# Written order on VectorE, ScalarE and Pool between two expert FFNs, with the routing in six pieces

## The chip, the cores and the metric

One core of one Trainium2 chip runs the kernel. The metric is device time in microseconds (us). TensorE is PE in the profile, VectorE DVE, ScalarE ACT, GpSimd POOL, and the engine that issues most transfers SP. Weight loads of TensorE have a row of their own, PEld.

## The reference

4096 tokens (16 sequences of 256) of width 256, all in float32. The layer is a macaron:

```
x = x + 0.5 * ffn(layernorm(x))     # first FFN
x = x + attention(layernorm(x))
x = x + 0.5 * ffn(layernorm(x))     # second FFN, same weights

ffn(h):  n = w_norm * rms_norm(h)
         probs = softmax(n @ w_router)               # 32 experts, top 4, 128 slots each
         each expert: (silu(g) * u) @ w_down         # hidden width 176
         shared:  sigmoid(n @ w_sg) * ((silu(n @ sw_gate) * (n @ sw_up)) @ sw_down)   # hidden width 704
         return h + weighted experts + shared
attention: 16 query heads, 8 key/value heads of 32, rotary, 50*tanh(s/50), causal softmax
```

## The kernel before

x stays in SBUF as 32 tiles of 128 tokens; four tiles make a **group**, so there are eight groups. The stages, in the order in which they are written:

- **First FFN, routing.** `route(n, g)` (L209) is a generator that is advanced piece by piece. `moments` (L197) takes mean and variance (DVE `st`, `mv`) and a power on POOL (`s`). Then come the normalised rows `xr` (DVE, L230), the rescaled residual `x` (ACT, L233, which overwrites what `xr` reads), transposes `pt` on PE, their copies `xnT` (ACT), router logits `pl` (PE), `lg` and `ex` (DVE, ACT), and the top-4 chain from `tot` to `mask` (DVE, L262 to L279) with a write of `xr` to the DRAM table `xtab` (SP). `rows` has two buffers for `xr`.
- **Slots** (L284) turn the masks into token indices; **experts** (L369) gather rows, run three products and scatter-add into the DRAM sum `acc`.
- **Sums and projections.** `project(pool, g)` (L427) reads `acc` back (`a`, one buffer), adds it to x on POOL (L423), takes the moments, normalises (`h`, ACT, L443), transposes (`pta`, PE), and makes q, k and v: six products `pq` (PE, L456), each turned by a shuffle `qs` and a product with the cosines on DVE (L459, L463; `qs` has two buffers) and two operations on POOL (L464, L465), and two products `pv` copied to `v` by DVE (L488).
- **Attention** is a loop over **units** `k = 4g + j`, j = 0..3: group g, one of its two sequences, one half of the heads. A unit issues wide scores `sc` (PE), tanh and exp on ACT (L512, L515), a causal select on POOL (L517); for odd j the output product `poa` and its addition to x (DVE, L560); some projection products of group g+1; narrow scores `sc`; then denominators `den` and values `y` of the unit before, whose DVE steps run from `dT` to `yT` (L541 to L546). Scores and the shared FFN's `pg` live in one PSUM pool, `big`, of two buffers: a unit's narrow scores wait for the tanh of its wide ones. Most other products use the pool tag `mm`, also two buffers.
- **Fill.** The shared FFN (`shared`, L332: `pg` on PE, tanh on ACT, two steps `act` on DVE, `po` on PE) has no deadline. `fill.take(us)` issues that many us of it wherever PE would wait; the constants on L44 say how much.
- **Second FFN**, as the first; the routing of groups 0 to 6 is advanced inside the attention loop.

The order of instructions on PE is the written one (`manual_schedule`, L95). On DVE, ACT, POOL and SP a scheduler has chosen it when the program was built. [...]

In the attention loop, per group, the pieces stand as follows (before): routing of group g-1 in j = 1 (moments), j = 2 and j = 3 (xr, x and transposes, half each), and of g-2 in j = 0 (logits) and j = 1 (top-4 chain). Group g+2's projection: j = 1 sum, j = 2 moments, j = 3 `h` and transposes. Group g+1's products: j = 0 three `pq`, j = 1 two `pv`, j = 2 three `pq`.

The lines that the order turns on:

```
ORDERED = {mybir.EngineType.PE}
ROUTE_FILL, SLOT_FILL, FIRST_FILL, EXPERT_FILL, SUM_FILL, PROJECT_FILL = 2.2, 2.5, 6.0, 2.4, 14.0, 2.0
SPARE = (1.0, 0.0, 3.0, 4.0)
PROJECT_PIECES = ((2, 1), (0, 2), (2, 1), (0, 0))
```

Of the kernel before, what the change touches and what calls it, by code (L numbers as in the profile page):

```python
# [13 lines left out]
ALU = mybir.AluOpType  # L14
# [22 lines left out]
QK_SCALE = 256.0 ** -0.5  # L37
TINY = float(np.finfo(np.float32).tiny)
XW = C + E
ORDERED = {mybir.EngineType.PE}  # L40

ROUTE_FILL, SLOT_FILL, FIRST_FILL, EXPERT_FILL, SUM_FILL, PROJECT_FILL = 2.2, 2.5, 6.0, 2.4, 14.0, 2.0  # L44
SPARE = (1.0, 0.0, 3.0, 4.0)
PROJECT_PIECES = ((2, 1), (0, 2), (2, 1), (0, 0))

# [40 lines left out]
def macaron_kernel(ctx: ExitStack, tc: tile.TileContext, X, Wq, Wk, Wv, Wo, w_norm, w_router, w_gate, w_up,  # L88
# [3 lines left out]
    of = out.rearrange("b t c -> (b t) c")  # L92


    ctx.enter_context(tc.manual_schedule(engines=ORDERED))  # L95
    cpool = ctx.enter_context(tc.tile_pool(name="consts", bufs=1))
    dram = ctx.enter_context(tc.tile_pool(name="dram", bufs=1, space=DRAM))
    stat = ctx.enter_context(tc.tile_pool(name="stat", bufs=3))
# [97 lines left out]

    def moments(g):  # L197

        mv = stat.tile([P, GT, 2], F32, name="mv")
        for t in range(GT):  # L200
            st = stat.tile([P, 6], F32, name="st")
            nc.vector.bn_stats(st, x[:, g * GT + t, :])
            nc.vector.bn_aggr(mv[:, t, :], st)
        s1 = stat.tile([P, GT], F32, name="s1")
        nc.gpsimd.tensor_scalar_add(s1, mv[:, :, 1], LN_EPS)
        nc.gpsimd.tensor_tensor(s1, s1, power, ALU.pow)
        return mv, s1

    def route(n, g):  # L209

        mv, s1 = moments(g)
        s2 = stat.tile([P, GT], F32, name="s2")
        nc.gpsimd.tensor_mul(s2, s1, s1)
        nc.gpsimd.tensor_mul(s2, s2, mv[:, :, 1])
        nc.gpsimd.tensor_scalar_add(s2, s2, RMS_EPS)
        nc.gpsimd.tensor_tensor(s2, s2, power, ALU.pow)
        nc.gpsimd.tensor_mul(s2, s2, s1)
        xa = stat.tile([P, GT], F32, name="xa")
        nc.gpsimd.tensor_scalar(xa, s1, 0.5, 1.0, ALU.mult, ALU.add)
        xb = stat.tile([P, GT], F32, name="xb")  # L220
        nc.gpsimd.tensor_mul(xb, s1, mv[:, :, 0])
        nc.gpsimd.tensor_scalar_mul(xb, xb, -0.5)
        xr = rows.tile([P, GT, XW], F32, name="xr")
        yield 0.0
        for h in range(GT // 2):
            pt = ps1.tile([P, 2, 2, P], F32, tag="mm", name="pt")
            for j in range(2):
                t = 2 * h + j
                i = g * GT + t
                nc.vector.tensor_scalar(  # L230
                    xr[:, t, 0:C], x[:, i, :], mv[:, t, 0:1], s2[:, t : t + 1], ALU.subtract, ALU.mult
                )
                nc.scalar.activation(  # L233
                    x[:, i, :], x[:, i, :], AF.Identity, bias=xb[:, t : t + 1], scale=xa[:, t : t + 1]
                )
                for c in range(2):
                    nc.tensor.transpose(pt[:, c, j, :], xr[:, t, c * P : (c + 1) * P], ident)
            i0 = (g * GT + 2 * h) * P
            for c in range(2):
                nc.scalar.activation(  # L240
                    xnT[:, c, i0 : i0 + 2 * P], pt[:, c].rearrange("p j t -> p (j t)"), AF.Identity,
                    scale=wnorm[:, c : c + 1],
                )
            yield 0.5
        pl = ps1.tile([P, GT, E + 1], F32, tag="mm", name="pl")
        for t in range(GT):
            i = g * GT + t
# [36 lines left out]
    def slots(pool, idx, q):  # L284
# [6 lines left out]
            nc.tensor.matmul(pc[:NT, e, :], lhsT=mask[:, q * EG + e, :], rhs=triu, start=True, stop=True)  # L291
        cum = pool.tile([NT, EG, P + 1], F32, name="cum")
        nc.scalar.copy(cum[:, :, 0:P], pc[:NT])
        cnt = pool.tile([NT, EG], F32, name="cnt")
        nc.vector.tensor_copy(cnt, cum[:, :, P - 1])
        yield 0.5
# [14 lines left out]
        nc.vector.tensor_tensor(past, iota, hi.unsqueeze(2).to_broadcast([NT, EG, CAP]), ALU.is_ge)  # L311
        nc.gpsimd.tensor_sub(sel, sel, past)
        nc.vector.tensor_add(cum[:, :, 0:P], cum[:, :, 0:P], lo.unsqueeze(2).to_broadcast([NT, EG, P]))
        nc.vector.tensor_copy(cum[:, :, P : P + 1], const("base", NT).unsqueeze(1).to_broadcast([NT, EG, 1]))
        yield 0.2
        row = pool.tile([P, EG], F32, name="row")
        for e0 in range(0, EG, 3):
# [109 lines left out]
    def project(pool, g):  # L427


        add_sums(g, read_sums(pool, 0, g, 1))  # L430
        yield 0.0
        mv, s1 = moments(g)
        hb = stat.tile([P, GT], F32, name="hb")
        nc.gpsimd.tensor_mul(hb, s1, mv[:, :, 0])
        nc.gpsimd.tensor_scalar_mul(hb, hb, -1.0)
        yield 0.0
        hT = pool.tile([P, 2, GW], F32, name="hT")
        for p in range(GT // 2):
            pt = ps1.tile([P, 2, 2, P], F32, tag="mm", name="pta")
            for j in range(2):  # L440
                t = 2 * p + j
                h = rows.tile([P, C], F32, name="h")
                nc.scalar.activation(  # L443
                    h, x[:, g * GT + t, :], AF.Identity, bias=hb[:, t : t + 1], scale=s1[:, t : t + 1]
                )
                for c in range(2):
                    nc.tensor.transpose(pt[:, c, j, :], h[:, c * P : (c + 1) * P], ident)
# [150 lines left out]
    def feed_forward(n, pool, works, fill):  # L598


        for g in works:
            fill.take(ROUTE_FILL)
            next(works[g])
            if g + 1 in works:
                next(works[g + 1])
            for _ in works[g]:
                fill.take(ROUTE_FILL)
            fill.ready = g + 1
        if n == 0:
            clear(0)  # L610
# [16 lines left out]
    proj = ExitStack()  # L627
    with tc.tile_pool(name="ffn0", bufs=1) as pool:
        first = {g: route(0, g) for g in range(NG)}
        next(first[0])  # L630
        feed_forward(0, pool, first, fill)
        clear(1)
        pp = proj.enter_context(tc.tile_pool(name="proj", bufs=1, side="right", reuse_waits="tile"))
        projects = {0: project(pp, 0)}
        next(projects[0])
        fill.take(SUM_FILL)
        next(projects[0])
        fill.take(FIRST_FILL)
        for _ in projects[0]:
            fill.take(PROJECT_FILL)  # L640
        fill.finish(2)
        projects[1] = project(pp, 1)
        for _ in range(4):
            next(projects[1])
            fill.take(PROJECT_FILL)

    def store(i, tiles=1):
        nc.sync.dma_start(
# [15 lines left out]
    with tc.tile_pool(name="attn", bufs=1, reuse_waits="tile") as pool:  # L664
# [5 lines left out]
        for k in range(len(units) + 2):  # L670
# [18 lines left out]
            spare_time(SPARE[j])  # L689
            advance(projects.get(g + 1), PROJECT_PIECES[j][1])  # L690

            if j < 2 and g >= 2:
                advance(routing[g - 2])
                fill2.ready = g - 2 + j
            elif j >= 2:
                advance(routing.get(g - 1))
            if j == 1:
                if g >= 1:
                    routing[g - 1] = route(1, g - 1)
                    next(routing[g - 1])  # L700
                if g + 2 < NG:
                    projects[g + 2] = project(pp, g + 2)
                    next(projects[g + 2])
            if j == 2 and g + 2 < NG:
                fill.finish(g + 3)
                next(projects[g + 2])
            if j == 3:
                advance(projects.get(g + 2), 2)
    proj.close()

    with tc.tile_pool(name="ffn1", bufs=1, reuse_waits="tile") as pool:
# [36 lines left out]
```

## Time and profile before

| what | value |
|---|---|
| three runs | 1242.18, 1249.54 (median), 1250.28 us |
| profiled execution | 1249.98 us, span on the core 1248.3 us |
| mean granted TensorE clock | 0.958 |
| DVE busy | 615.6 us (49%) |
| ACT busy | 419.4 us (34%) |
| POOL busy | 501.9 us (40%) |
| chain that ended last | PE 73%, DVE 10%, POOL 6%, ACT 4%, DMA 4% |

The span can be cut by what PE works on: routing 0 to 123 us, slots to 235, experts to 403, sums and first projections to about 463, attention to 920, the second FFN's slots to 1040, its experts and the end to 1248. Idle time of an engine counts only where another one, in the end PE, waits for it.

### The profile page before, as it was taken

How to read it: one execution, taken by the hardware profiler on the slowest of the kernel's cores; microseconds unless marked ns; L12 is line 12 of the kernel's file. 1: busy time of each engine (PE TensorE's matmuls, PEld its weight loads, DVE VectorE, ACT ScalarE, POOL GpSimd, SP SyncE). 2: the span in 40 equal slices, each digit the busy share in tenths (PEclk: the TensorE clock that was granted, in tenths of full speed). 3: DMA queues.
4: the chain of work that ended last, by engine and by line, in shares of the span. 5: the costliest groups of instructions: out<-in, count | busy, mean ns of one | idle time of the engine just before them, and what ended most of it. 6: DMA issues, size and time to landing. Idle time of an engine off the chain costs nothing.

```text
span 1248.3 us, 15475 instructions
## 1 busy us (share of the span) xinstructions
PE 1134.2 (91%) x5408; PEld 652.9 (52%) x5408; DVE 615.6 (49%) x1621; ACT 419.4 (34%) x761; POOL 501.9 (40%) x590
## 2 busy tenths in 40 slices
PE   6899999999999589898989898989779999999998
PEld 4466545666665344444444454544354555657564
DVE  5655654444343334546464646554356474343434
ACT  3333010222121036665555555655511102122211
POOL 4500120345452477656264645452211112445435
PEclk9799898999999899998989899999889999999999
DMA  8413200577777220000000000000020004677748
GB/s 269 123 39 116 80 19 0 108 145 155 149 154 199 72 67 1 1 1 20 1 20 1 20 1 19 1 20 19 2 66 25 19 1 86 147 153 151 153 81 273
DMA packets 137805, 92.92 MB, mean 74 GB/s; under 512 B 80448, under 2 KB 135040, under 8 KB 137728
## 3 DMA queue, kind: packets, MB, share of 16 engines
q1 hardware_dynamic: 125440, 74.11, 21.4%
q0 software_dynamic: 12288, 17.83, 8.7%
q8 instruction: 43, 0.70, 0.2%
q14 instruction: 34, 0.28, 0.1%
HBM read 60.94 MB, written 30.97 MB: 74 GB/s over the span
## 4 chain that ended last, share of the span: by engine, by line
PE 73%; DVE 10%; POOL 6%; ACT 4%; DMA 4%; issue 2%; SPq 0%; POOLq 0%; DVEq 0%; ACTq 0%
PE pg L349 21%; PE po L361 15%; PE pge L396 7%; PE pq L456 7%; PE poe L408 5%; PE sc L505 3%; PE poa L556 3%; PE pl L249 3%; PE den L538 2%; PE y L538 2%; PE pte L388 2%; DMA a<-acc 2%; POOL x L423 1%; DMA xg<-xtab,idx 1%; PE pa L321 1%
## 5 line engine op out<-in xcount | busy, mean ns | idle before, releaser
L349 PE MATMUL pg<-xnT,sw 128*128 128x512 f32 x704 | 329.2, 613 | 13.0 <-DVE act L355 8.8
L361 PE MATMUL po<-swd,act 128*128 128x256 f32 (+1 forms) x768 | 208.3, 416 | 13.2 <-DVE act L355 8.1
L349 PEld LDWEIGHTS pg<-xnT,sw 128*128 128x128 f32 x704 | 129.9, 194 | 164.9 <-issue 143.9
L411 POOL DMA_INDIRECT acc<-y,idx x64 | 101.4, 1585 | 249.1 <-DVE y L410 205.4
L361 PEld LDWEIGHTS po<-swd,act 128*128 128x128 f32 (+1 forms) x768 | 144.0, 200 | 71.1 <-issue 31.9
L353 ACT ACTIVATE act<-pg 128x512 f32<-128x512 f32 x96 | 57.3, 597 | 317.3 <-PE pg L349 317.3
L517 POOL TENSOR_SCALAR_AFFINE_SELECT p<-p 128x512 f32<-128x512 f32 x128 | 80.4, 638 | 162.1 <-ACT p L515 158.6
L354 DVE SCALAR_TENSOR_TENSOR act<-act,pg 128x512 f32<-128x512 f32 x96 | 65.4, 682 | 150.2 <-ACT act L353 150.1
L512 ACT ACTIVATE p<-sc 128x512 f32<-128x512 f32 (+1 forms) x128 | 102.2, 801 | 61.3 <-PE sc L505 60.6
L515 ACT ACTIVATE p<-p 128x512 f32<-128x512 f32 (+1 forms) x128 | 107.6, 843 | 3.5
L396 PE MATMUL pge<-xgT,wgu 128*112 128x128 f32 (+1 forms) x768 | 95.6, 274 | 2.2 <-issue 2.2
L381 POOL DMA_INDIRECT xg<-xtab,idx x64 | 68.1, 1064 | 62.4 <-DVE idx L327 43.5
L396 PEld LDWEIGHTS pge<-xgT,wgu 128*112 128x112 f32 (+1 forms) x768 | 88.6, 182 | 4.9 <-issue 4.9
L365 DVE SCALAR_TENSOR_TENSOR x<-po,sg,x 128x256 f32<-128x256 f32 x64 | 30.9, 483 | 119.1 <-PE po L361 119.0
L408 PE MATMUL poe<-wd,sie 112*128 112x256 f32 (+1 forms) x256 | 78.6, 405 | 0.8 <-DVE sie L403 0.8
L505 PE MATMUL sc<-qT,kT 32*128 32x256 f32 (+1 forms) x512 | 65.3, 537 | 11.8 <-ACT p L512 9.7
L391 ACT ACTIVATE xgT<-pte,wnorm 128x128 f32<-128x128 f32 x128 | 39.8, 364 | 101.8 <-PE pte L388 101.6
L464 POOL TENSOR_TENSOR qs<-qs,kc 128x512 f32<-128x512 f32 x48 | 61.2, 1274 | 29.7 <-DVE qs L459 29.7
L456 PE MATMUL pq<-hT,wk 128*128 128x512 f32 x64 | 40.7, 769 | 28.7 <-DVE v L488 26.4
L355 DVE TENSOR_TENSOR act<-act,pg 128x512 f32<-128x512 f32 x96 | 65.6, 683 | 2.3
L456 PE MATMUL pq<-hT,wq 128*128 128x512 f32 x128 | 65.3, 636 | 0.9 <-DVE kT L463 0.9
L556 PE MATMUL poa<-wo,yT 128*128 128x256 f32 x256 | 59.5, 385 | 0.0
(110 smaller groups left out, 1384.2 us busy)
## 6 DMA issues: line engine op xcount, KB each, us to landing
xtab<-xr SPq DMA_DIRECT2D x16, 576.0 KB
acc<-zero SPq DMA_DIRECT2D x2, 4224.0 KB
a<-acc SPq DMA_DIRECT2D x16, 512.0 KB
wgu<-in_L_ffn_w_gate SPq DMA_DIRECT2D x64, 112.0 KB
wgu<-in_L_ffn_w_up SPq DMA_DIRECT2D x64, 112.0 KB
wd<-in_L_ffn_w_down SPq DMA_DIRECT2D x64, 112.0 KB
x<-in_L_attn_X SPq DMA_DIRECT2D x8, 512.0 KB
wgu<-in_L_ffn_w_gate SPq DMA_DIRECT2D x64, 64.0 KB
```

Source lines behind the costliest of these rows:

```text
L349: nc.tensor.matmul(pg[:, s, :], lhsT=sw[:, c, w0 : w0 + P], rhs=xnT[:, c, cols], start=(c == 0), stop=(c == 1))
L361: nc.tensor.matmul(po, lhsT=act[:fw, k, t * P : (t + 1) * P], rhs=swd[:fw, k, :], start=(k == 0), stop=(k == len(FC) - 1),)
L381: nc.gpsimd.indirect_dma_start(out=xg, out_offset=None, in_=xtab[n], in_offset=bass.IndirectOffsetOnAxis(ap=idx[:, e : e + 1], axis=0), bo ...
L396: nc.tensor.matmul(pg[:fw, n_, :], lhsT=wgu[:, c, w0 : w0 + fw], rhs=xgT[:, c, :], start=(c == 0), stop=(c == 1))
L408: nc.tensor.matmul(po, lhsT=si[:fw, k, :], rhs=wd[:fw, k, :], start=(k == 0), stop=(k == 1))
L411: nc.gpsimd.indirect_dma_start(out=acc[n], out_offset=bass.IndirectOffsetOnAxis(ap=idx[:, e : e + 1], axis=0), in_=y, in_offset=None, boun ...
L456: nc.tensor.matmul(pq, lhsT=weights[:, c, :], rhs=hT[:, c, :], start=(c == 0), stop=(c == 1))
L505: nc.tensor.matmul(sc[i // 2][:, i % 2, 0 : 2 * w].rearrange("p (s t) -> p s t", s=2), lhsT=kT[r, m, t0 + k0 : t0 + k0 + P], rhs=qT[r, m, ...
L512: nc.scalar.activation(parts[h], sc[h][:, :, 0 : 2 * w], AF.Tanh, scale=QK_SCALE / SOFTCAP)
L515: nc.scalar.activation(parts[h], parts[h], AF.Exp, scale=SOFTCAP)
L517: nc.gpsimd.affine_select(out=diag, in_=diag, compare_op=ALU.is_ge, fill=0.0, base=0, pattern=[[0, 4], [1, P]], channel_multiplier=-1,)
L556: nc.tensor.matmul(po, lhsT=yT[:, c // 2, c % 2, qh * P : (qh + 1) * P], rhs=wo[:, c // 2, c % 2, :], start=(c == 0), stop=(c == 3),)
```

## The change

For DVE, ACT and POOL the written order replaces the scheduler's, from the end of the first FFN's experts to the end of the attention loop; outside, it stays with the scheduler. Routing has six pieces instead of five: moments; `xr` and `x`; one half's transposes; the other's; logits; top-4 chain. In the attention loop each open routing advances by one piece per unit: group g-1 has its moments in j = 1, `xr` and `x` in j = 2, transposes in j = 3 and the next group's j = 0, logits in j = 1, the top-4 chain in j = 2. In a projection the read of the sums, the addition, the moments, the normalising (now into the tile `a` that held the sums) and two transposes are pieces of their own; in the loop group g+2 has its addition in j = 0, moments in j = 1, normalising in j = 2, transposes in j = 3. In the first FFN's routing, moments and `xr` are written up to two groups ahead. Three fill constants change, small statistics tiles get five buffers, and a constant column of `cum` is copied earlier.

```diff
-ROUTE_FILL, SLOT_FILL, FIRST_FILL, EXPERT_FILL, SUM_FILL, PROJECT_FILL = 2.2, 2.5, 6.0, 2.4, 14.0, 2.0
+ROUTE_FILL, SLOT_FILL, FIRST_FILL, EXPERT_FILL, SUM_FILL, PROJECT_FILL = 3.0, 2.5, 6.0, 2.4, 17.0, 1.5
...
+        yield 0.0
         xr = rows.tile([P, GT, XW], F32, name="xr")
+        for t in range(GT):
+            i = g * GT + t
+            nc.vector.tensor_scalar(
+                xr[:, t, 0:C], x[:, i, :], mv[:, t, 0:1], s2[:, t : t + 1], ALU.subtract, ALU.mult
+            )
+            nc.scalar.activation(
+                x[:, i, :], x[:, i, :], AF.Identity, bias=xb[:, t : t + 1], scale=xa[:, t : t + 1]
+            )
         yield 0.0
         for h in range(GT // 2):
             pt = ps1.tile([P, 2, 2, P], F32, tag="mm", name="pt")
             for j in range(2):
                 t = 2 * h + j
-                i = g * GT + t
-                nc.vector.tensor_scalar(
-                    xr[:, t, 0:C], x[:, i, :], mv[:, t, 0:1], s2[:, t : t + 1], ALU.subtract, ALU.mult
-                )
-                nc.scalar.activation(
-                    x[:, i, :], x[:, i, :], AF.Identity, bias=xb[:, t : t + 1], scale=xa[:, t : t + 1]
-                )
...
-        add_sums(g, read_sums(pool, 0, g, 1))
+        a = read_sums(pool, 0, g, 1)
+        yield 0.0
+        add_sums(g, a)
         yield 0.0
         mv, s1 = moments(g)
...
         yield 0.0
+
+        for t in range(GT):
+            nc.scalar.activation(
+                a[:, t, :], x[:, g * GT + t, :], AF.Identity, bias=hb[:, t : t + 1], scale=s1[:, t : t + 1]
+            )
+        yield 0.0
...
-        for g in works:
+        for g, work in works.items():
+            later = [works.get(g + d) for d in range(3)]
+            next(work)
+            if g == 0:
+                next(later[1])
             fill.take(ROUTE_FILL)
-            next(works[g])
-            if g + 1 in works:
-                next(works[g + 1])
-            for _ in works[g]:
-                fill.take(ROUTE_FILL)
+            next(work)
+            advance(later[1])
+            fill.take(ROUTE_FILL)
+            next(work)
+            advance(later[2])
+            fill.take(ROUTE_FILL)
+            next(work)
             fill.ready = g + 1
...
+        ordered = ExitStack()
+        ordered.enter_context(tc.manual_schedule(engines={ET.DVE, ET.Activation, ET.Pool}))
         pp = proj.enter_context(tc.tile_pool(name="proj", bufs=1, side="right", reuse_waits="tile"))
         projects = {0: project(pp, 0)}
         next(projects[0])
         fill.take(SUM_FILL)
+        advance(projects[0], 2)
+        fill.take(FIRST_FILL)
         next(projects[0])
-        fill.take(FIRST_FILL)
-        for _ in projects[0]:
-            fill.take(PROJECT_FILL)
+        fill.take(PROJECT_FILL)
+
+        advance(projects[0], 2)
         fill.finish(2)
         projects[1] = project(pp, 1)
-        for _ in range(4):
-            next(projects[1])
+        for k in range(8):
+            advance(projects[1], 1 if k < 4 else 0)
+            advance(projects[0])
             fill.take(PROJECT_FILL)
+        advance(projects[1], 2)
+        projects[2] = project(pp, 2)
+        next(projects[2])
...
-            if j < 2 and g >= 2:
-                advance(routing[g - 2])
-                fill2.ready = g - 2 + j
-            elif j >= 2:
-                advance(routing.get(g - 1))
-            if j == 1:
-                if g >= 1:
-                    routing[g - 1] = route(1, g - 1)
-                    next(routing[g - 1])
...
+            if j == 1 and g >= 1:
+                routing[g - 1] = route(1, g - 1)
+
+            for r, work in routing.items():
+                next(work, None)
+                if k - 4 * r == 9:
+                    fill2.ready = r + 1
+
+            fill.finish(min(g + 3, NG))
+            advance(projects.get(g + 2), 2 if j == 3 else 1)
+            if j == 3 and g + 3 < NG:
+                projects[g + 3] = project(pp, g + 3)
+                next(projects[g + 3])
+        advance(routing[NG - 2])
+        advance(routing[NG - 1])
+        fill2.ready = NG - 1
+        ordered.close()
```

More of the change, by code (lines that the diff above doesn't have):

```diff
@@ L39 @@
 XW = C + E
-ORDERED = {mybir.EngineType.PE}
-ROUTE_FILL, SLOT_FILL, FIRST_FILL, EXPERT_FILL, SUM_FILL, PROJECT_FILL = 2.2, 2.5, 6.0, 2.4, 14.0, 2.0
+ET = mybir.EngineType
+ROUTE_FILL, SLOT_FILL, FIRST_FILL, EXPERT_FILL, SUM_FILL, PROJECT_FILL = 3.0, 2.5, 6.0, 2.4, 17.0, 1.5
 SPARE = (1.0, 0.0, 3.0, 4.0)
@@ L92, in macaron_kernel @@
     of = out.rearrange("b t c -> (b t) c")
-    ctx.enter_context(tc.manual_schedule(engines=ORDERED))
+    ctx.enter_context(tc.manual_schedule(engines={ET.PE}))
     cpool = ctx.enter_context(tc.tile_pool(name="consts", bufs=1))
@@ L197, in moments @@
     def moments(g):
-        mv = stat.tile([P, GT, 2], F32, name="mv")
+        mv = stat.tile([P, GT, 2], F32, name="mv", bufs=5)
         for t in range(GT):
@@ L203, in moments @@
             nc.vector.bn_aggr(mv[:, t, :], st)
-        s1 = stat.tile([P, GT], F32, name="s1")
+        s1 = stat.tile([P, GT], F32, name="s1", bufs=5)
         nc.gpsimd.tensor_scalar_add(s1, mv[:, :, 1], LN_EPS)
@@ L211, in route @@
         mv, s1 = moments(g)
-        s2 = stat.tile([P, GT], F32, name="s2")
+        s2 = stat.tile([P, GT], F32, name="s2", bufs=5)
         nc.gpsimd.tensor_mul(s2, s1, s1)
@@ L217, in route @@
         nc.gpsimd.tensor_mul(s2, s2, s1)
-        xa = stat.tile([P, GT], F32, name="xa")
+        xa = stat.tile([P, GT], F32, name="xa", bufs=5)
         nc.gpsimd.tensor_scalar(xa, s1, 0.5, 1.0, ALU.mult, ALU.add)
-        xb = stat.tile([P, GT], F32, name="xb")
+        xb = stat.tile([P, GT], F32, name="xb", bufs=5)
         nc.gpsimd.tensor_mul(xb, s1, mv[:, :, 0])
         nc.gpsimd.tensor_scalar_mul(xb, xb, -0.5)
+        yield 0.0
         xr = rows.tile([P, GT, XW], F32, name="xr")
+        for t in range(GT):
[6 more added lines that the diff above has]
+            )
         yield 0.0
@@ L293, in slots @@
         nc.scalar.copy(cum[:, :, 0:P], pc[:NT])
+        nc.vector.tensor_copy(cum[:, :, P : P + 1], const("base", NT).unsqueeze(1).to_broadcast([NT, EG, 1]))
         cnt = pool.tile([NT, EG], F32, name="cnt")
@@ L313, in slots @@
         nc.vector.tensor_add(cum[:, :, 0:P], cum[:, :, 0:P], lo.unsqueeze(2).to_broadcast([NT, EG, P]))
-        nc.vector.tensor_copy(cum[:, :, P : P + 1], const("base", NT).unsqueeze(1).to_broadcast([NT, EG, 1]))
         yield 0.2
@@ L441, in project @@
                 t = 2 * p + j
[L442 to L445, printed above, removed]
                 for c in range(2):
-                    nc.tensor.transpose(pt[:, c, j, :], h[:, c * P : (c + 1) * P], ident)
+                    nc.tensor.transpose(pt[:, c, j, :], a[:, t, c * P : (c + 1) * P], ident)
             nc.scalar.copy(
@@ L629, in macaron_kernel @@
         first = {g: route(0, g) for g in range(NG)}
-        next(first[0])
+        advance(first[0], 2)
         feed_forward(0, pool, first, fill)
         clear(1)
+        ordered = ExitStack()
+        ordered.enter_context(tc.manual_schedule(engines={ET.DVE, ET.Activation, ET.Pool}))
         pp = proj.enter_context(tc.tile_pool(name="proj", bufs=1, side="right", reuse_waits="tile"))
@@ L690, in macaron_kernel @@
             advance(projects.get(g + 1), PROJECT_PIECES[j][1])
-            if j < 2 and g >= 2:
-                advance(routing[g - 2])
-                fill2.ready = g - 2 + j
-            elif j >= 2:
-                advance(routing.get(g - 1))
-            if j == 1:
-                if g >= 1:
-                    routing[g - 1] = route(1, g - 1)
-                    next(routing[g - 1])
[L701 to L708, printed above, removed]
+            if j == 1 and g >= 1:
[13 more added lines that the diff above has]
+        ordered.close()
     proj.close()
```

## The prediction

> **What bounds the kernel.** I read first the page's engine row, then the busy times by stage, then PE's waits stage by stage, then the timeline around the longest.
>
> ```profile
> PE 1134.2 (91%) x5408; PEld 652.9 (52%) x5408; DVE 615.6 (49%) x1621; ACT 419.4 (34%) x761; POOL 501.9 (40%) x590
> ```
>
> PE is the bound, and the change leaves its work alone: the same matmuls, in another order. What can be won or lost is PE's idle time, 1248.3 - 1134.2 = 114.1 us, and the time at half clock that follows idle time. By stage (window less PE busy): routing 19.6, slots 6.5, experts 2.3, sums and first projections 18.4 (403 to 470), attention 47.8 (470 to 920), second slots 12.6, the rest 6.9. The written order covers 403 to 920: 66 us.
>
> PE's waits in 580 to 700 us, two groups of the attention (us in total, times, longest):
>
> ```profile
> PE pq L456 <- DVE v L488: 10.0, 2, 5.0
> PE pta L447 <- ACT h L443: 3.0, 2, 1.5
> ```
>
> That is all the idle time there: one wait of 5.0 and one of 1.5 us per group. The timeline shows how the first arises:
>
> ```profile
> 639.94 1.33 DVE L230 TENSOR_SCALAR xr<-x,mv,s 128x256 f32<-128x256 f32 x2 [3.16 <-POOL s L217]
> 644.42 1.28 DVE L488 COPY v<-pv 128x512 f32<-128x512 f32 x2
> 645.15 3.78 PE L456 MATMUL pq<-hT,wk 128*128 128x512 f32 x4 [5.01 <-DVE v L488]
> ```
>
> DVE stands 3.16 us for POOL's statistics, then does xr and the chain to yT; v, which frees the PSUM for pq, is behind them. And pq itself then runs at half clock: two products take 5.4 to 6.7 us after this wait, 3.63 without it.
>
> The sums (403 to 440) are the same fault, larger:
>
> ```profile
> 415.70 0.43 DVE L202 BATCH_NORM_STATS2 st<-x 128x6 f32<-128x256 f32 x1 [9.79 <-POOL x L423]
> 416.76 7.09 PE L349 MATMUL pg<-xnT,sw 128*128 128x512 f32 x12 [8.78 <-DVE act L355]
> 429.99 8.30 PE L361 MATMUL po<-swd,act 64*128 64x256 f32 x26 [3.73 <-DVE act L355]
> ```
>
> The statistics stand ahead of the fill's act on DVE and wait for sums that land at 413.3; the fill that should cover the wait is shut out by it.
>
> A fourth place, in the last group, shows what a wait on ACT costs:
>
> ```profile
> 878.93 1.66 DVE L230 TENSOR_SCALAR xr<-x,mv,s 128x256 f32<-128x256 f32 x4 [4.26 <-POOL s L217]
> 879.65 0.60 ACT L233 ACTIVATE x<-x,xb,xa 128x256 f32<-128x256 f32 x1 [3.64 <-DVE xr L230]
> 883.21 1.22 PE L505 MATMUL sc<-qT,kT 32*128 32x256 f32 x4 [5.25 <-ACT p L512]
> 885.21 1.22 PE L505 MATMUL sc<-qT,kT 32*128 32x256 f32 x4 [0.78 <-ACT p L512]
> 886.36 1.94 PE L538 MATMUL den<-p,ones 128*32 128x512 f32 x8
> ```
>
> x waits for xr, the tanh is behind x, the narrow scores behind the tanh: 5.25 + 0.78 us, and den and y then take 5.2 us where 2.7 is usual.
>
> [...]den above runs 1.94 against 1.07. [...]the subtraction L258 takes 1.14 us beside POOL and 0.29 without it. I therefore take DVE's durations from places where POOL is busy.
>
> **The change, part by part.**
>
> *Sums: gain.* Written order puts the fill's act ahead of the statistics, and SUM_FILL brings 3.5 pg and two po first. In the old order PE ended its last expert at 397.42; one more pg (3.53) now falls before that, so 400.95. Then 14 pg matmuls of 0.88 to 413.3, po 2.85 twice to 419.1. The sums are there at 409.4 + 3.9 (DMA) + 2.35 (POOL) = 415.7; DVE takes the statistics at 419.7 to 421.4, POOL 1.75, ACT four normalisings at 0.55 to 425.5. PE meanwhile does two more po to 424.8, then pta, and pq starts at about 427.0. Before: 443.53. Gain 16.5, which is the stalls 8.78 + 3.73 + 1.02 and about 4 of half clock, less one. The scatters whose end sets 409.4 are chained by their own transfers (3.9 each), so the later poe costs nothing. From pq to the first sc I count 20 us (before 19.6): POOL is the bound there, six turned products at 2.55 each, one sum, statistics.
>
> *First group: gain 2.* POOL no longer adds all eight sums in one go (eight times 2.35 from 413 to 461) but one per group. The reads on SP wait for the transposes that free a; they are issued a unit before their use and take 3.9 us, so they are covered by a unit of about 14 us. The xtab writes behind them on SP have a unit too.
>
> *Attention, groups 2 to 5: a wait goes and another comes.* The stall on v goes: v is now at the head. But follow DVE from the start of pv in j = 1 (t = 0). yT 2.3; v 2.9 and 4.5; logits (pl ends 5.55) lg to ex 2.0 to 7.65; eight statistics 3.3 to 10.95; two turned products 2.6 to 13.55; dT to yT 2.55 to 16.1. PE: sc 6.6, two pq 10.25, sc 10.9, den and y 13.6, a fill pg 17.15, third pq 19.0; no stall so far. DVE act follows pg's tanh: 17.95 to 19.35; then the third turned product 20.65, top-4 chain 3.74 to 24.4, xr from 24.4 (0.66 each). ACT has x (4 of 0.55) behind xr, then the four normalisings of group g+2 (2.2), and only then the tanh of unit j = 3: 25.1 + 2.2 + 2.2 + 1.0 = 30.5. PE has in between sc and poa alone, to 23.8. It stands 6.6 us, 0.7 more for the second half of the narrow scores, and then at half clock (about 2.5, as at 883). Behind ACT's x also stand the exps, and behind those POOL's selects; these have a unit to spare. A further wait of 0.7 stays at pta behind xnT. Per group 6.6 + 0.7 + 0.7 + 2.5 = 10.5; before 5.0 + 1.5 + 2.0 to 3.0, about 8.6. Loss 2 per group, four groups: 8.
>
> *Groups 1, 6, 7.* Group 1 has no top-4 chain: stall 3.3 + 0.7 + 0.7 + clock 2 against 2.79 + 1.47 + 1.8: loss 1. Group 6 has no group 8 to normalise: 4.6 + 0.7 + 2.5 against 4.38 + 1.8: loss 1.5. Group 7 had 9.4 of stalls (853 to 897), and I count 9.0: nothing.
>
> *Second FFN's start.* poa, statistics, POOL (4.1), xr, pt as before (6.53 idle), with pl now in front of lg on DVE: 0.7 more; and one po instead of two between logits and slots: 1.5. Loss 2.
>
> *First routing and slots: loss 2 (between a gain of 4 and a loss of 6).* The first transposes of group 1 now stand before the first pg (xr at 19.3, PE free at 17.0: 2.3 idle), and group 2's come a pg earlier though its xr waits for the first xtab write in any case (38.9): about 0.5 more. A stall of 1.47 at 55 goes. The slots start one pg sooner after the last mask (1). Half clock here (10 us at 38, 14 at 144) can fall otherwise; no row tells.
>
> *Nothing:* five buffers for statistics (no wait on them in the trace), the earlier constant column of cum (no PE wait names it), total fill (only moved; 31 us of it remain after the last expert in both).
>
> Sum: -16.5 - 2 + 8 + 1 + 1.5 + 2 + 2 = -4.0. Span 1244.3; the profiled execution was 1249.98, so 1246.0. The median shown is 0.44 lower than that execution; I stay at 1246.
>
> **Rivals.**
>
> *The block on ACT does not form* (0.24). If DVE gets to xr some 6.5 us sooner than I count, all stalls of groups 1 to 6 go: 47 of stall and clock, less 3.5 at pta, plus the other terms: about 1192; with half of it left 1215. For: DVE is busy only 49%, and these times hold POOL's interference, which the top-4 chain's 3.74 would lose without it (about 2.6). Against: the chain hangs on PE's own third pq; from its end 1.3 + 3.74 + 0.7 + 4.4 + 1.0 = 11.1 us pass against 4.8 of PE work.
>
> *POOL joins the chain: slower* (0.19). In j = 2 POOL has fourteen small operations behind the statistics (4.1 + 2.0, from 9.35 to 15.5), two selects (16.8) and the first turned product (19.3). DVE's third shuffle reuses that product's qs buffer and is due at 19.35: no margin. Each us POOL is later delays xr, ACT and PE by one, in four groups[...]. At 3 us late: 4 x 4.7 = 19, so 1265. Over 1 us late it outweighs the gain.
>
> *The order is not what it says*: excluded; the built program's list has xr, x, normalising and tanh in just this order.
>
> **How the numbers follow.** Likeliest 0.57, its own range 1236 to 1256; no block 0.24 (1192 to 1236); POOL late 0.19 (1256 to 1275). The 8-in-10 range 1218 to 1264 leaves out about 0.10 on each side. A measurement can tell about 1%, 12.5 us: below 1237 0.25, above 1262 0.14, between 0.61.
>
> **What would show it.** Right: no PE wait over 2 us between 400 and 430; no pq waiting for v; in groups 2 to 5 one wait of narrow sc for ACT p of 5.5 to 8 us in j = 3, with ACT x idle before it for DVE xr. Wrong: no such wait (first rival), or DVE qs waiting for POOL kT in j = 2 with sc waits over 9 us (second). Most doubtful is DVE's time between statistics and xr.

## The result and the profile after

The changed kernel takes 1240.62 us (median of 11 runs, 1236.49 to 1245.03) against 1246.96 for the kernel before in the same rounds (1242.18 to 1252.63): ratio 0.9945, 95% interval 0.9923 to 0.9967. The difference is real and smaller than the one per cent that the forecast called noticeable. The profiled execution of the changed kernel took 1237.82 us with a span of 1236.1, 2.8 us under its median; that of the kernel before lay 3.0 us over its own. So the two traces differ by 12.2 us where the medians differ by 6.3; the six between them are found below, in the first FFN.

The engine row of the page after:

```profile
PE 1124.1 (91%) x5408; PEld 646.2 (52%) x5408; DVE 612.0 (50%) x1621; ACT 405.3 (33%) x761; POOL 501.6 (41%) x590
```

The same 5408 matmuls as before. They took 10.1 us less, and PE stood at half clock for less of the time (78 us of the span after, 104 before, granted clock 0.50 there); its idle time, 1236.1 - 1124.1 = 112.0, is what it was, 2 us less. A small difference, then, but not for want of change. PE's waits in 580 to 700 us, the view that the prediction shows of before (total, times, longest; line numbers are each kernel's own):

```profile
PE sc L511 <- ACT p L518: 13.0, 2, 6.5
PE pta L453 <- ACT xnT L242: 1.1, 2, 0.5
```

Of before's two lines, 13.0 us in all, neither is left; 14.1 us stand under two other names. The wait of pq for v is gone from every group. The timeline of the same group as before shows what came instead (start and duration in us; in brackets the idle time before and what ended it):

```profile
637.16 3.72 PE L562 MATMUL poa<-wo,yT 128*128 128x256 f32 x16
640.84 2.41 DVE L227 TENSOR_SCALAR xr<-x,mv,s 128x256 f32<-128x256 f32 x4
642.38 2.08 ACT L230 ACTIVATE x<-x,xb,xa 128x256 f32<-128x256 f32 x4 [7.77 <-DVE xr L227]
644.36 2.06 ACT L443 ACTIVATE a<-x,hb,s 128x256 f32<-128x256 f32 x4
646.32 1.91 ACT L518 ACTIVATE p<-sc 128x1024 f32<-128x1024 f32 x2
647.38 2.13 PE L511 MATMUL sc<-qT,kT 32*128 32x256 f32 x8 [6.49 <-ACT p L518]
649.44 1.94 PE L544 MATMUL den<-p,ones 128*32 128x512 f32 x8
```

Read it upwards. The narrow scores need the PSUM that ACT's p (the tanh of the wide scores) empties. The inputs of that p have stood ready since the wide scores ended at 637.23, but ACT's list has x at its head, which idles 7.77 us for DVE's xr, and nothing behind it starts in that time. Next come four normalisings `a`, whose inputs were there long before (in group 2 since 567.20, while they run at 579.61). And den takes 1.94 us instead of 1.07: from 646.20 to 653.02 the granted clock is 0.50.

The waits at the sums ahead of the attention are gone. After the first FFN's last expert the lines now run:

```profile
397.10 12.28 PE L351 MATMUL pg<-xnT,sw 128*128 128x512 f32 x28
409.22 11.92 PE L363 MATMUL po<-swd,act 128*128 128x256 f32 x48
415.62 0.42 DVE L202 BATCH_NORM_STATS2 st<-x 128x6 f32<-128x256 f32 x1
423.18 1.98 PE L462 MATMUL pq<-hT,wk 128*128 128x512 f32 x4 [0.67 <-ACT hT L454]
```

The sums land at 412.34 (POOL's add, 410.00 and 2.34 long), DVE takes their statistics only at 415.62, behind the fill's act and the additions of its first two po, and PE has fill up to 421.07 without a break. The longest wait before the first pq is 0.67 us; before it was 8.78.

### The profile page after: what moved, and what is told of

The parts are those of the page before. It is cut to its first block, busy times and chain, and to the rows that moved or that the text cites. A ratio compares the mean times of both kernels' runs of the same rounds, so it can differ in the third digit from the quotient of the medians.

```text
span 1236.1 us, 15506 instructions
## 1 busy us (share of the span) xinstructions
PE 1124.1 (91%) x5408; PEld 646.2 (52%) x5408; DVE 612.0 (50%) x1621; ACT 405.3 (33%) x761; POOL 501.6 (41%) x590
## 4 chain that ended last, share of the span: by engine, by line
PE 51%; DMA 18%; issue 13%; DVE 10%; ACT 5%; POOL 3%; POOLq 0%; ACTq 0%; DVEq 0%
DMA acc<-y,idx 17%; PE pg L351 14%; PE po L363 7%; PE pq L462 6%; PE sc L511 4%; PE den L544 3%; PE poa L562 3%; PE y L544 3%; PE pv L490 2%; PE pl L251 2%; DVE act L356 1%; ACT x L230 1%; PE den L542 1%; DVE act L357 1%; PE y L542 1%
## 5 line engine op out<-in xcount | busy, mean ns | idle before, releaser
L363 PE MATMUL po<-swd,act 128*128 128x256 f32 (+1 forms) x768 | 198.1, 401 | 7.6 <-DVE row L327 3.1
L363 PEld LDWEIGHTS po<-swd,act 128*128 128x128 f32 (+1 forms) x768 | 138.3, 192 | 61.1 <-issue 29.1
L511 PE MATMUL sc<-qT,kT 32*128 32x256 f32 (+1 forms) x512 | 75.3, 560 | 44.6 <-ACT p L518 42.2
L518 ACT ACTIVATE p<-sc 128x512 f32<-128x512 f32 (+1 forms) x128 | 96.5, 804 | 33.4 <-PE sc L511 32.9
L521 ACT ACTIVATE p<-p 128x512 f32<-128x512 f32 (+1 forms) x128 | 100.8, 843 | 0.0
L547 DVE STREAM_TRANSPOSE dT<-den 128x512 f32<-128x512 f32 x32 | 22.9, 717 | 109.1 <-PE den L542 109.1
L511 PEld LDWEIGHTS sc<-qT,kT 32*128 32x128 f32 x512 | 27.4, 194 | 80.5 <-ACT p L518 51.0
L230 ACT ACTIVATE x<-x,xb,xa 128x256 f32<-128x256 f32 x64 | 33.7, 591 | 87.6 <-DVE xr L227 73.7
## 6 DMA issues: line engine op xcount, KB each, us to landing
wgu<-in_L_ffn_w_gate SPq DMA_DIRECT2D x64, 112.0 KB
wgu<-in_L_ffn_w_up SPq DMA_DIRECT2D x64, 112.0 KB
wd<-in_L_ffn_w_down SPq DMA_DIRECT2D x64, 112.0 KB
```

What stands on the lines that cost most here:

```text
L363: nc.tensor.matmul(po, lhsT=act[:fw, k, t * P : (t + 1) * P], rhs=swd[:fw, k, :], start=(k == 0), stop=(k == len(FC) - 1),)
L511: nc.tensor.matmul(sc[i // 2][:, i % 2, 0 : 2 * w].rearrange("p (s t) -> p s t", s=2), lhsT=kT[r, m, t0 + k0 : t0 + k0 + P], rhs=qT[r, m, ...
L518: nc.scalar.activation(parts[h], sc[h][:, :, 0 : 2 * w], AF.Tanh, scale=QK_SCALE / SOFTCAP)
L521: nc.scalar.activation(parts[h], parts[h], AF.Exp, scale=SOFTCAP)
```

## The experiments

Ten kernels were run. Two lengths hold most of the answer, so they are given here once for all of them, from each one's trace: from the end of the first FFN's last poe (an expert's last product) to the second group's first pv (kernels with the old fills do 3.5 us of shared work in it that the others have done earlier), and from there to the attention's last poa. The runs fell into several rounds, in which the median of the kernel before was 1245.8 to 1247.0.

| Kernel | Written order | last poe to second pv | second pv to last poa | Time, median |
|---|---|---|---|---|
| before | none | 81.8 | 439.6 | 1245.8 to 1247.0 |
| e2: old pieces | before the attention | 80.6 | 439.9 | 1244.37 |
| e10: old pieces | in the attention | 71.4 | 476.0 | 1275.75 |
| e1: new pieces | none | 82.4 | 436.9 | 1251.01 |
| e5: new pieces | before the attention | 75.7 | 436.9 | 1244.63 |
| e12: new pieces | to the first group's end | 63.4 | 436.1 | 1230.07 |
| after: new pieces | all of it | 61.7 | 445.9 | 1240.62 |
| e3: newest routing first | all of it | 61.6 | 429.7 | 1228.89 |
| e6: x one step later | all of it | 61.7 | 390.0 | 1189.09 |
| e4: x and a later | all of it | 64.2 | 391.9 | 1189.43 |
| e8: e4 and fill moved | all of it | 64.3 | 391.9 | 1188.55 |
| e11: x one step later | before the attention | 77.1 | 437.4 | 1245.95 |

**e1: the pieces without the order.** The line that sets DVE, ACT and POOL in written order is left out of the changed kernel:

```diff
-        ordered.enter_context(tc.manual_schedule(engines={ET.DVE, ET.Activation, ET.Pool}))
```

> The changed kernel without the written order on VectorE, ScalarE and Pool; the six pieces, the weaving and the larger fills stay. Theory (the gain before the attention is the order's, the loss in the attention is the pieces'): the statistics of the first group's sums stand ahead of the fill's act on VectorE again, so TensorE waits 8 to 9 us for act near 408 and pq starts 14 to 18 us later than the 423.2 of the changed kernel; the four normalisings x stay one block on ScalarE, so the narrow scores' waits of 5.4 to 7.4 us in groups 1 to 5 stay. Time about 1255, 1250 to 1260. Rival (the order itself makes the block on ScalarE hurt, because the clips can't slip past it): those waits fall to under 3 us each, some 20 us less in groups 1 to 5, and the time is 1232 to 1242.

Measured: 1251.01 us, 1.0040 of before (1.0025 to 1.0055). PE waits 6.50 us for act at 408, pq starts 9.7 us later than in the changed kernel where the theory had 14 to 18, and by the second group's pv 20.9 us are lost: more than the theory said, over a longer stretch than it named. The time fell into its range, but in the attention it was wrong. There the rival had the waits right, which are gone from groups 1 to 6, and not the time: only 9 us came back, since another wait of each group took over:

```profile
PE pl L251 <- DVE v L494: 13.9, 3, 4.7
```

(PE's waits between 540 and 720.) The timeline has it:

```profile
572.25 0.69 DVE L227 TENSOR_SCALAR xr<-x,mv,s 128x256 f32<-128x256 f32 x1 [4.24 <-POOL s L217]
576.35 1.28 DVE L494 COPY v<-pv 128x512 f32<-128x512 f32 x2
577.09 3.62 PE L251 MATMUL pl<-wr,xnT 128*128 128x33 f32 x16 [4.64 <-DVE v L494]
```

That is the fault of the kernel before, at much the same length: free of the order, the scheduler puts xr as early as it may, DVE stands for POOL's statistics, and v is behind it.

**e2: the order without the pieces.** The kernel before, with this line ahead of its sums and its end just ahead of the attention:

```diff
         clear(1)
+        ordered = ExitStack()
+        ordered.enter_context(
+            tc.manual_schedule(engines={mybir.EngineType.DVE, mybir.EngineType.Activation, mybir.EngineType.Pool})
+        )
...
+        ordered.close()
```

> The kernel before, with VectorE, ScalarE and Pool in written order only from the first FFN's last expert to the attention's first step; nothing else changed. Theory (the order alone takes away the wait of 8.78 us for act and those that follow it): pq starts at 426 to 429 instead of 443.5, the attention is as before, and the time is 14 to 18 us under the kernel before, about 1231. Rival (the larger fill and the woven pieces are needed too): less than 8 us under it, with a wait of TensorE over 5 us left between 400 and 430.

Measured: 1244.37 us, 0.9975 (0.9954 to 0.9996): the gain of 14 to 18 us isn't there, and the rival's time, less than 8 us gained, is. Its first half came as expected: from the last poe to pq 29.3 us instead of 46.0, 16.7 less. But then:

```profile
438.87 2.34 POOL L423 TENSOR_TENSOR x<-x,a 128x1024 f32<-128x1024 f32 x1
441.24 0.43 DVE L202 BATCH_NORM_STATS2 st<-x 128x6 f32<-128x256 f32 x1 [6.09 <-POOL x L423]
445.54 1.09 ACT L443 ACTIVATE h<-x,hb,s 128x256 f32<-128x256 f32 x2 [25.99 <-POOL hb L435]
446.19 1.18 PE L447 MATMUL pta<-kc,h 128*128 128x128 f32 x4 [12.49 <-ACT h L443]
```

The second group's sum is written down after all six turned products of the first, so POOL comes to it at 438.87, and PE stands 12.49 us for what hangs on it, from 433.70, a little later than the rival named; the trace shows the clock halved for 20.48 us from 435.73 on (on the page, the slice from 434 to 465 has a granted clock of 0.6). In the changed kernel POOL has that sum at 428.59, between the turned products, because the second group's pieces are written between those of the first. Order alone, on this stretch, brings the time forward and gives it back; the new pieces and fills alone (e1) bring nothing.

**e3: the newer routing first.** In the third step of a group:

```diff
-            for r, work in routing.items():
+            for r, work in sorted(routing.items(), reverse=j == 2):
```

> The changed kernel, but in the third step of each group the two routings advance newest first, so that VectorE writes the four xr of the group behind before the top-4 chain of the group before that. Theory (ScalarE's block waits for xr, which VectorE reaches late): xr is done some 4 us earlier, the narrow scores' waits of 6.3 to 7.4 us in groups 2 to 5 fall to 2 to 3.5 us, and the time falls by 14 to 22 us, half-clock windows after the waits included: 1219 to 1227. Rival (the wait is for the sums' add or the rotation of k, so for Pool, or comes back when the delayed top-4 chain holds the shuffles): the sum of TensorE's waits in groups 2 to 5 falls by less than 6 us and the time by less than 8.

Measured: 1228.89 us, 0.9852 (0.9812 to 0.9892), 11.7 under the changed kernel by the medians, 14.2 by the spans. The direction is the theory's, the size below its 14 to 22 us by the medians: the waits of groups 2 to 5 are 3.70, 3.70, 4.17 and 4.62 us, where 2 to 3.5 was expected. They are 10.5 us less in sum, so the rival is out. In group 2:

```profile
572.35 3.83 DVE L227 TENSOR_SCALAR xr<-x,mv,s 128x256 f32<-128x256 f32 x4
576.22 0.60 ACT L230 ACTIVATE x<-x,xb,xa 128x256 f32<-128x256 f32 x1 [0.68 <-DVE xr L227]
576.73 2.06 ACT L443 ACTIVATE a<-x,hb,s 128x256 f32<-128x256 f32 x4
```

The four xr start 3.7 us earlier than in the changed kernel (576.09 there) but take 3.83 us instead of 2.41: they now run beside POOL's turned products and selects, and the last of them ends at 576.18, 0.15 us after POOL's turned product of 574.73 to 576.03. In the changed kernel the first, beside POOL's qT, takes 1.44 us and ends 0.15 us after it, and the other three, beside which POOL has only a copy of 0.35 us, take 0.40 each.

**e4 and e6: x out of the clips' way** (the clips are ACT's tanh over the scores). In e6 only ACT's four x move, from the piece of xr to that of the second transposes:

```diff
-            nc.scalar.activation(
-                x[:, i, :], x[:, i, :], AF.Identity, bias=xb[:, t : t + 1], scale=xa[:, t : t + 1]
-            )
...
+            for t in range(GT if h else 0):
+                i = g * GT + t
+                nc.scalar.activation(
+                    x[:, i, :], x[:, i, :], AF.Identity, bias=xb[:, t : t + 1], scale=xa[:, t : t + 1]
+                )
```

e4 moves the normalisings a as well, behind the narrow scores:

```diff
+            if j == 3:
+                advance(projects.get(g + 2))
...
-            advance(projects.get(g + 2), 2 if j == 3 else 1)
+            advance(projects.get(g + 2), (1, 1, 0, 2)[j])
```

> The changed kernel, but ScalarE normalises x one step later, after the second transposes' xnT, and the normalising a of the group two ahead stands in the fourth step behind its narrow scores instead of in the third: no block of eight activations stands ahead of a clip any more. Theory (that block is what the attention loses): the narrow scores' waits on ScalarE in groups 1 to 6 fall from 5.4 to 7.4 us to under 1.5 us each, with the half-clock windows that follow them; 35 to 50 us less, 1190 to 1205. Rival (VectorE or Pool is as late and TensorE waits for qT, v or xr in its place): waits of as many us under other names, and less than 15 us gained.

> The changed kernel with only ScalarE's x moved one step later, behind the second transposes' xnT; the normalising a stays where it was, ahead of the narrow scores' clips. Theory (what costs is that x waits for VectorE's late xr with the clips queued behind it, not that eight activations take 4 us): a has its inputs some 6 us before the clips are due, so nothing waits for it, the narrow scores' waits fall under 1 us, and the time is as with both moved, 1187 to 1195. Rival (the length of the block matters): waits of 2 us stay in each of groups 1 to 6, with half-clock windows after some, 1200 to 1212.

Measured: e4 1189.43 us, 0.9536 (0.9497 to 0.9574); e6 1189.09 us, 0.9543 (0.9509 to 0.9577). Both theories hold, e4's with 51 us where 35 to 50 was expected. PE's waits of e6 between 540 and 720, all of them:

```profile
PE pta L455 <- ACT xnT L239: 1.4, 3, 0.5
PE po L365 <- DVE x L568: 0.3, 1, 0.3
```

and the same place of group 2:

```profile
564.65 2.06 ACT L445 ACTIVATE a<-x,hb,s 128x256 f32<-128x256 f32 x4
566.94 1.94 ACT L520 ACTIVATE p<-sc 128x1024 f32<-128x1024 f32 x2 [0.23 <-PE sc L513]
570.95 0.71 PE L513 MATMUL sc<-qT,kT 32*128 32x256 f32 x8
571.00 3.05 DVE L227 TENSOR_SCALAR xr<-x,mv,s 128x256 f32<-128x256 f32 x4
571.60 1.06 PE L546 MATMUL den<-p,ones 128*32 128x512 f32 x8
```

xr starts 5.24 us after the wide scores start (565.76), in the changed kernel 5.21 (570.88 and 576.09): it is as late as ever, and nobody waits for it, because p is now ahead of what needs it. The four a take their 2.06 us while ACT would have idled. So the four a cost nothing where nothing ahead of them waits, and e4, which moves them too, is no faster. What costs is that an instruction at the head of the list waits for another engine; behind it the length counts as well, since x and a take 4.04 us between xr and p in the changed kernel (577.62 to 581.66). Groups 2 to 5 are 9.6, 9.7, 8.9 and 11.1 us shorter than in the changed kernel. For group 2 that is the wait, 6.48, and the half clock from 581.34 to 588.17, of which 5.55 us lie behind the wait and, at a granted clock of 0.50, cost half of it, 2.8: together 9.3 of the 9.6. The edit changes the first FFN's routing too, which reaches the last poe at 400.25 instead of 397.17.

**e8: fill ahead of the second FFN's first transposes,** on top of e4:

```diff
+        if n:
+            fill.take(6.0)
         for g, work in works.items():
```

> The variant with x and a moved (1189 us), and 6 us of the shared expert put ahead of the second FFN's first transposes, which wait 7.4 us for xr after the attention. If that wait is on the path and the shared work left over at the end (31 us) is longer than what must hide there, 4 to 7 us less: 1182 to 1186, with the wait at the first pt near 1 us. Rival (the sums' reading and adding at the end, some 20 us of Pool, becomes the end): 1187 to 1190.

Measured: 1188.55 us, 0.9535 (0.9503 to 0.9567). The rival was right. The wait at the first pt falls from 7.40 to 1.84 us, the time stays: of the shared work behind the last expert 24 us are left instead of 31, and the last po still ends at 1179.56 (1181.22 in e4), the span 7.2 us after it instead of 3.9. What closes the span there is the adding of the last sums, not PE:

```profile
1164.26 16.55 POOL L427 TENSOR_TENSOR x<-x,a 128x1024 f32<-128x1024 f32 x7 [6.15 <-DMA a<-acc]
1179.04 2.06 DVE L681 TENSOR_TENSOR x<-x,a 128x256 f32<-128x256 f32 x1
1181.52 0.42 DVE L681 TENSOR_TENSOR x<-x,a 128x256 f32<-128x256 f32 x1
```

POOL adds seven groups' sums up to 1180.81; DVE's own addition beside it takes 2.06 us, the last one, after it, 0.42.

**e10: the order in the attention on the old pieces.** The kernel before, with the order of e2 set around the attention's loop instead.

> The kernel before, with VectorE, ScalarE and Pool in written order in the attention's loop alone; its pieces, weaving and fills are as before. Theory (written order is only as good as the pieces it writes down; the old pieces hold xr, x, h just ahead of the transposes that need them): TensorE waits for xr in the routing's transposes and for h in the projections', 2 to 5 us each, two or three times in a group; the attention grows by 20 to 60 us: 1265 to 1305. Rival (the order alone costs what the changed kernel's attention lost, the pieces nothing): 1250 to 1260, with the waits at the narrow scores as in the changed kernel.

Measured: 1275.75 us, 1.0235 (1.0201 to 1.0269). The theory holds: the attention from the second pv on grows by 36 us, and PE's waits between 540 and 720 are those of the old pieces, which write xr and h just ahead of the transposes that need them; those for h are shorter than expected.

```profile
PE pt L237 <- DVE xr L230: 16.0, 4, 5.5
PE pta L447 <- ACT h L443: 8.1, 6, 1.6
```

Up to the second pv this kernel is 10 us shorter than before. POOL adds two groups' sums ahead of the attention, at 407.55 and 414.30, and the third at 466.36, where in the kernel before it adds all eight by 461.51, between the turned products. The act that PE awaited 3.73 us behind the third group's statistics is there after 0.62, and up to the second pv PE idles 12.8 us instead of 20.8. So some of the gain comes by the loop's order alone, on the old pieces.

**e5, e12: how far the order is needed.** The changed kernel with `ordered.close()` moved ahead of the attention's loop (e5), or into its second group (e12):

```diff
         for k in range(len(units) + 2):
             g, j = divmod(k, 4)
+            if k == 5:
+                ordered.close()
```

> The changed kernel, but the written order on VectorE, ScalarE and Pool ends where the attention's loop begins; in the attention these engines go by the scheduler again. Runs so far: order alone on the stretch before the attention gave 16.7 us to the first pq and lost them again to one wait of 12.5 us for the second group's normalising (order without weaving), and weaving without order gave nothing to the first group either. Theory (order and weaving are worth 16 to 20 us only together, and the order costs the attention some 9 us): from the last poe of the first FFN to the second group's pv as in the changed kernel, 61 to 64 us against 82; from there to the last poa 436 to 440 against 446; 1230 to 1236. Rival (the order within the attention's first group is needed as well): 70 us or more from the last poe to the second group's pv and 1240 to 1250.

> The changed kernel with the written order on VectorE, ScalarE and Pool ending after the first group's four steps and one of the second's. Theory (order and weaving gain 20 us together between the last poe and the second group's pv, and the order is needed to the first group's end for it; from there on the order costs 9 us): 61 to 63 us from the last poe to the second group's pv, 436 to 440 from there to the last poa, 1228 to 1236. Rival (what the first group gains under the order is lost in the second when the scheduler takes over): 440 or more after it and 1238 or more.

Measured: e5 1244.63 us, 0.9981 (0.9967 to 0.9996); its theory falls, its rival was right: 75.7 us to the second pv, with two waits in the first group that the changed kernel hasn't (4.22 us of pq for kT at 450, 5.54 of the scores for p at 459). e12 1230.07 us, 0.9885 (0.9837 to 0.9932), as its theory says but for 0.4 us in the first length: 63.4 and 436.1. It keeps the one effect of the change, 15 us gained up to the second group (81.8 less 3.5, now 63.4), and leaves out the other, the 10 us that the order costs on these pieces behind it (445.9 against 436.1). The kernel before, with its old pieces, has 439.6 there.

**e11: x later, but free.** e6 with the order closed ahead of the attention.

> The variant with x alone moved (1189 us), but the written order on VectorE, ScalarE and Pool ends where the attention's loop begins. Theory (the gain of moving x exists only in a written order, since the free scheduler puts xr and x ahead of their step by itself: its lists for ScalarE have x before the clips again, and xr ahead of v on VectorE): the waits of 3 to 5 us of the router's transposes for v stay, from the second group's pv to the last poa 434 to 440 us, 1240 to 1247. Rival (moving x is worth as much without the order): under 400 us there and about 1200.

Measured: 1245.95 us, 1.0005 (0.9988 to 1.0021): nothing of e6's 51 us is left. The scheduler, given the later place, puts xr and x ahead again, as its theory had it, and the waits of pl for v are back (13.9 us between 540 and 720).

## Why the prediction was right

The forecast was 1246 with no difference of more than one per cent; measured was 1240.6, within the likeliest case's own range. Of the 5.4 us between them 3.0 lie in the execution that the forecast started from, which was that much over its median; the step itself was forecast as -4.0 and measured as -6.3. Its mechanism is what the traces show: one wait goes, another comes at the place named, and the sums' stalls vanish. Term by term, from the two profiled executions:

| Term | Forecast | Measured | How |
|---|---|---|---|
| Sums | -16.5 | -16.5 | last poe to pq 46.0, now 26.0; less the 3.5 of pg done before |
| First pq to the end of the first group | -2 | -1.6 | 78.04, now 76.49 |
| Group 1 | +1 | +2.6 | 49.89, now 52.44 |
| Groups 2 to 5 | +8 | +7.1 | 244.91, now 251.96 |
| Groups 6 and 7 | +1.5 | -1.8 | 102.54, now 100.71 |
| Second FFN | +2 | +2.0 | last poa to the end 329.37, now 331.32 |
| First routing and slots | +2 | -3.9 | to the last poe 397.49, now 397.17, with 3.5 of pg more |
| Sum | -4.0 | -12.2 | spans 1248.3 and 1236.1 |

*Sums.* The forecast had pq 26.05 us after the last poe; it was 26.01. The first wait that it didn't name lies just behind: pv for qT, 4.15 us at 430.32, and it is why pq to the first score took 21.9 instead of the 20 counted. The first group gave those 2 us back.

*Groups 2 to 5.* The wait was put at 6.6 us in each; it is 6.48, 6.49, 6.32 and 7.41, in the step named, with ACT's x idle 7.8 to 12.5 us for xr ahead of it. Counted from the start of pv, the forecast had the tanh end at 30.5 us; the scores resumed at 30.5, 30.5, 31.2 and 30.5. Inside that chain, in group 2, two errors cancelled: the first xr took 1.44 us and not 0.66, the eight activations 4.04 and not 4.4. "Block does not form" is out: the waits are there, and e6 shows what their absence is worth, 51 us, close to the 1192 us forecast for that case. "POOL joins the chain" is out too: POOL's kT ended at 570.96 in group 2, DVE's third shuffle followed at 571.23 right behind its act, and no wait of DVE for POOL stands there. That is a margin of 0.3 us, as thin as feared. The 4.7 us a group in that case are 3 of delay and 1.7 of further half clock; that the 1.7 would come with it was the author's estimate, and no run shows it.

*Group 1* was under-counted: its wait is 5.43 us, not 3.3, with 6.83 us of half clock from 523.32, 2 us before its end. *Groups 6 and 7*: group 6's wait, 4.47, is the 4.6 forecast, but group 7's came to 6.2 us in six small waits, where 9.0 had been counted as in before. The 5.25 us wait shown of before in the last group has shrunk to 1.44.

*First routing and slots* is the one term off by more than 4 us: +2 forecast, -3.9 by the two traces. But e2 and e10, whose first FFN is that of the kernel before, reach the last poe at 390.28 and 391.77, while before's profiled execution took 397.49; the changed kernel's first FFN reaches it at 397.17, and at 395.84 to 397.32 in the four kernels (e1, e3, e5, e12) that leave that stage untouched. Against the mean of e2 and e10 the term is 397.17 - 391.03 - 3.53 = +2.6, as forecast. What was off was the execution that the sum was made against, 6 us longer in that stage than its like (34 us of half clock before 235 us, 17 in e2; in the second slice of their pages the granted clock is 0.7 and 0.8). Up to 380 us e2 has the same lists of instructions as before on PE, DVE, ACT and POOL. With that put right the terms add up to -5.7, beside -6.3 of the medians. How close the sum comes is luck in part: groups 6 and 7 came out 3.3 us under their term, group 1 came out 1.6 over, and the comparison for the first FFN rests on two executions that lie 1.5 us apart.

So some 16 us were won up to the second group; 6 of them were lost in the attention behind it (439.6, now 445.9) and 4 to 5 in the two FFNs. The forecast named all three. It did not ask whether an effect belongs to one part of the change alone. e1, e2 and e5 show that the whole gain needs the order to the first group's end and the new pieces and fills under it. e10 shows that the old pieces get about 10 us of it from the order in the loop. Two kernels that would part this further were not run: the old pieces with the order over both stretches, and the larger fills by themselves. e1 and e12 show that the loss is that of the order on these pieces; e6 shows that it hangs on the place of four activations.

## What to carry to other kernels

In this kernel a written order made every instruction's place a promise: what waits for another engine has to stand behind what is ready and needed. So, having set an order, list for each engine the instructions that idle, and look at what is queued behind each; here moving four activations one step was worth eight times as much as the whole change (51 us against 6), and under the scheduler nothing (e11). And where order alone undoes a fault, look for the next group's work that was written behind it: in e2, 16.7 us gained at one place were lost at the next.

One profiled execution can lie several microseconds off in a stage that nobody touched; two kernels that share the stage tell.

## What the runs showed of the hardware that was not expected

In the traces of before and after, the length of a wait does not tell how much half clock comes with it. In the kernel before, three of PE's waits for v are alike, 5.02, 5.01 and 5.01 us up to 581.26, 645.15 and 704.38. The trace has 6.83 us of half clock at each, but from 580.59, 642.03 and 703.47 on, so PE works 6.16, 3.71 and 5.92 us under it. At the shorter waits of 2.79, 4.16 and 4.38 us (up to 529.15, 767.55 and 825.54) it lasts 3.41 us each time, from 529.39, 768.33 and 826.35; the wait of 1.47 us at 550.84 has none. In the changed kernel five waits of 4.47 to 6.49 us in groups 1 to 4 and 6 have 6.83 us each, and group 5's, 7.41 us, has 10.24. At the longest wait, 12.49 us in e2, the half clock lasted 20.48 us from 2 us after the wait's start, so some 10 us beyond its end, with two waits of about 1 us in them. What a wait costs beyond its own length has to be read at its place in the trace.

Four xr, the same operation on the same shapes, took 1.38 us in e4 ahead of the second FFN, with four operations of 0.19 to 0.43 us on POOL beside them, 2.41 us in the changed kernel's group 2, and 3.05 us in e6 and 3.83 us in e3, with POOL in turned products and selects of 0.64 to 1.30 us for most of that time. In the attention loops of before and after, 19 of 56 single xr take 0.69 to 1.46 us, and each of these ends 0.09 to 0.15 us after an operation of POOL; the other 37 take 0.37 to 0.41. The forecast's 0.66 us for one lies between the two.
